# Two groups of four graphs at a time in layer 1's aggregation and weighted sum

## The chip, the cores and the metric

The kernel runs on one NeuronCore of a Trainium2 chip. The metric is the device time of one execution in microseconds (us), as a median over several runs; one further execution was recorded by the hardware profiler. The engines are TensorE (PE in the profile; its weight loads are PEld), VectorE (DVE), ScalarE (ACT), GpSimd (POOL) and SyncE (SP), which here only issues DMAs. [...]

## What is computed

128 graphs of 128 nodes with 256 features, all in fp32. Layer 0 is a gated network (convolution of 17 taps, messages between nodes, a GRU gate) on all nodes. Layer 1 works on the first 25 nodes only, in five overlapping groups of nodes, and is the part that is changed:

```python
GROUPS = [list(range(25)), list(range(9)), [0, 9, 10, 11, 12, 13, 14],
          [6, 7, 8, 12, 13, 14], [3, 4, 5, 9, 10, 11]]

def _graph_conv(x, adj, W, b):
    A = adj + eye(n)
    dinv = rowsum(A) ** -0.5            # 0 where the sum is 0
    norm_adj = dinv[:, :, None] * A * dinv[:, None, :]
    return relu(norm_adj @ (x @ W) + b)

h = relu(layernorm(x))
for g, idx in enumerate(GROUPS):
    hid = _graph_conv(h[:, idx], adj[:, idx][:, :, idx], W1[g], b1[g])    # 256 -> 512
    o = _graph_conv(hid, adj[:, idx][:, :, idx], W2[g], b2[g])            # 512 -> 256
    fused[:, idx] += softmax(fusion_w)[g] * o
x = x + fused
```

The changed steps are the second aggregation, `relu(norm_adj @ (...) + b2)`, and the weighted sum `fused`.

## The kernel before

The 53 pairs of a group and one of its nodes (25 + 9 + 7 + 6 + 6) are called rows; a graph has 64 row places, so two graphs fill 128 partitions. Layer 1 goes in 8 blocks of 16 graphs. A block has four **quads** of four graphs (`q` = 0 to 3). The steps of a block (`block`, from L1081) are:

- py (L1093): x1h, the normalized features, times the matrix r4 gathers and scales each graph's rows into `yz`, one step for each quad.
- `first(g)` and `second(g)` (L1110, L1119): the products with W1 and W2 for the five groups of nodes, over all 16 graphs. Group 0 has 25 nodes, so 400 columns.
- `turn(q)` (L1136): four transposes (L1141) bring the quad's rows to partitions, in one PSUM bank pzt; ACT copies them to SBUF as zt (L1145).
- `gather(q)` (L1147): four fp32 matmuls of 64 rows by 64 columns (L1153) apply the normalized adjacency `ac` of each graph. A pair of graphs is indexed by a, a graph in it by s. The results of s go to the left half of one PSUM bank pg2[s]. DVE adds b2 into zt for each s (L1156), ACT takes the relu of both (L1157).
- `fuse(q)` (L1159): two matmuls (L1163) with s2w, which holds the weights of the five groups, sum the rows of a graph onto its nodes; DVE adds the result to x1 (L1165), and x1's quad is stored: by one DMA of POOL (L1168) in blocks 0 to 6, in block 7 by four DMAs of one graph each (L1172), from SP or, for some, ACT.

Beside it, `prepare(blk)` makes the normalized adjacency and r4 of a later block; pa (L1042), dd (L1063), pg (L1068, 512 columns), pr (L1073) and the copies to r4 (L1077) are its steps. All of these take their PSUM banks from the pool `ptmp`, five banks in rotation; layer 0's last stage, `stage_c`, takes most of its own from `pgat`, three banks.

`stage_c` handles layer 0's gates for one group of four graphs at a time, 32 in all, as a series of products (L755) with sums and gates on DVE and ACT between them. Its last seven steps use the weight `wn` and end in two tanh (L884); its results are finished and turned by DVE (L918 to L929, L936) and, for the last group, through PE (po, L899, with the copies zr, L893).

The order of the instructions of all engines is laid down when the kernel is built, by the class `Order`. Several lanes hold generators. Each step of a generator issues its instructions and yields two numbers, a cost and a wait: the planner's clock advances by the cost, and the generator is not due again until the wait is over. Among the lanes that have something due, the one with the least cost done for its weight is taken; if none is due, the clock jumps to the earliest. In the last part of the kernel the lanes are:

```python
order.run(loads, groups, beside, Lane([fetch(q) for q in range(NQ)], ahead=2),
          Lane([rows(q) for q in range(NQ)], ahead=2),
          Lane(second, ahead=2, weight=0.2))
```

`groups` holds the 32 `stage_c`, `second` the series prepare(0), block(0), prepare(1), block(1) and so on, of which two run at a time. A block may start when its preparation is done and the block before has passed its last gather (`B1_DONE`). The products of the last `wn` steps yield a cost of 0.87 and a wait of 0.2.

Of the kernel before, what the change touches and what calls it, by code (L numbers as in the profile page):

```python
# [9 lines left out]
FP = mybir.dt.float32  # L10
AF = mybir.ActivationFunctionType
# [4 lines left out]
B, N, D = 128, 128, 256  # L16
# [3 lines left out]
P = 128  # L20
GB = 4
# [9 lines left out]
SB = 16  # L31
QS = SB // GB
NBLK = B // SB
# [7 lines left out]
RP = 64  # L41
WIDE = 32
# [165 lines left out]
def kernel(ctx: ExitStack, tc: tile.TileContext, x, adj, consts, vecs, w_se, conv1_w,  # L208
                    conv2_w, w_msg, b_msg, w_ih, w_hh, W1, W2, b2, fusion_w, out):
    nc = tc.nc  # L210
# [7 lines left out]
    ptmp = ctx.enter_context(tc.tile_pool(name="ptmp", bufs=5, space=PSUM))  # L218
# [19 lines left out]
    def v(name, i=None):  # L238
        a, b = VAT[name]
        return vec[:, a:b] if i is None else vec[:, a + i:a + i + 1]  # L240
# [17 lines left out]
    s2w = cp.tile([P, 2 * WIDE], FP, name="s2w")  # L258
# [106 lines left out]
    lab, turn = ExitStack(), []  # L365
# [624 lines left out]
    def load_w1(n):  # L990

        if n < NBLK * NG:
            S["w1", n] = S["pool"].tile([P, 2, HID], FP, tag="w1", name=f"w1_{n}", bufs=2)
            nc.sync.dma_start(out=S["w1", n], in_=W1[n % NG].rearrange("(k p) o -> p k o", p=P))
# [86 lines left out]
    def block(blk):  # L1081
        while not (blk in P_DONE and blk - 1 in B1_DONE):
            yield 0.0, 0.5
        pool, yz, b2row = S["pool"], S["yz"], S["b2row"]
        w2, ac, r4 = S["w2"], S["ac"][blk % 2], S["r4"][blk % 2]

        for q in range(QS):
            while blk * QS + q not in R_DONE:
                yield 0.0, 0.5
            x1h = S.pop(("x1h", blk * QS + q))  # L1090
            py = ptmp.tile([P, 2, GB, NR], FP, tag="tmp", name=f"py{blk}_{q}")
            for cc in range(2):
                nc.tensor.matmul(py[:, cc], x1h[:, cc * P:(cc + 1) * P],  # L1093
                                 r4[:, q].rearrange("p j r -> p (j r)"), start=True, stop=True)
            nc.vector.tensor_copy(yz[:, 0, q * GB:(q + 1) * GB, :NR], py[:, 0])  # L1095
            nc.scalar.activation(yz[:, 1, q * GB:(q + 1) * GB, :NR], py[:, 1], AF.Copy)
            PY_DONE.add(blk * QS + q)
            yield 0.75, 0.0 if q < QS - 1 else 2.4

        hs = {}  # L1100

        def first(g):
            n, o = SIZES[g], OFFS[g]
            w1 = S.pop(("w1", blk * NG + g))
            hh = hs[g] = pool.tile([P, 4, SB, n], FP, tag="hh0" if g == 0 else "hh",
                                   name=f"hh{blk}_{g}", bufs=1 if g == 0 else 2)
            for m in range(4):
                ph = ptmp.tile([P, SB, n], FP, tag="tmp", name=f"ph1{blk}_{g}_{m}")
                for k in range(2):
                    nc.tensor.matmul(ph, w1[:, k, m * P:(m + 1) * P],  # L1110
                                     yz[:, k, :, o:o + n], start=(k == 0), stop=(k == 1))
                nc.scalar.activation(hh[:, m], ph, AF.Relu, bias=v("b1", g * 4 + m))  # L1112

        def second(g):
            n, o = SIZES[g], OFFS[g]
            for cc in range(2):
                pz = ptmp.tile([P, SB, n], FP, tag="tmp", name=f"pz1{blk}_{g}_{cc}")
                for m in range(4):
                    nc.tensor.matmul(pz, w2[:, g, m, cc * P:(cc + 1) * P], hs[g][:, m],  # L1119
                                     start=(m == 0), stop=(m == 3))  # L1120
                nc.vector.tensor_copy(yz[:, cc, :, o:o + n], pz)  # L1121

        for g in range(NG + 1):
            if g < NG:
                first(g)
                yield 5.5 if g == 0 else 1.95, 0.0
            if g:
                second(g - 1)
                yield 5.5 if g == 1 else 1.95, 0.0 if g < NG else 1.0
            if g < NG:  # L1130
                load_w1(blk * NG + g + 2)
        x1 = X1[blk]

        zts = {}

        def turn(q):  # L1136
            pz = ptmp.tile([P, 2, D], FP, tag="tmp", name=f"pzt{blk}_{q}")
            for a in range(2):
                for cc in range(2):
                    b0 = q * GB + 2 * a  # L1140
                    nc.tensor.transpose(  # L1141
                        pz[:, a, cc * P:(cc + 1) * P],
                        yz[:, cc, b0:b0 + 2, :].rearrange("p s r -> p (s r)"), ident)
            zt = zts[q] = pool.tile([P, 2, D], FP, tag="zt", name=f"zt{blk}_{q}", bufs=4)
            nc.scalar.activation(zt, pz, AF.Copy)  # L1145

        def gather(q):  # L1147
            zt = zts[q]
            pg2 = [ptmp.tile([P, D], FP, tag="tmp", name=f"pg2{blk}_{q}_{s}") for s in range(2)]
            for a in range(2):  # L1150
                for s in range(2):
                    rows = slice(s * RP, (s + 1) * RP)
                    nc.tensor.matmul(pg2[s][a * RP:(a + 1) * RP], ac[rows, 2 * q + a],  # L1153
                                     zt[rows, a], start=True, stop=True)
            for s in range(2):
                nc.vector.tensor_add(zt[:, s], pg2[s], b2row)  # L1156
            nc.scalar.activation(zt, zt, AF.Relu)  # L1157

        def fuse(q):  # L1159
            zt = zts.pop(q)  # L1160
            pf = ptmp.tile([P, D], FP, tag="tmp", name=f"pfu{blk}_{q}")
            for s in range(2):
                nc.tensor.matmul(pf[s * 2 * WIDE:(s + 1) * 2 * WIDE], s2w, zt[:, s],  # L1163
                                 start=True, stop=True)
            nc.vector.tensor_add(x1[:, q], x1[:, q], pf)  # L1165
            b0 = blk * SB + q * GB
            if blk < NBLK - 1:
                nc.gpsimd.dma_start(out=out[b0:b0 + GB, :WIDE], in_=x1[:, q])  # L1168
                return
            for j in range(GB):  # L1170
                eng = nc.scalar if q == QS - 1 and j % 2 else nc.sync
                eng.dma_start(out=out[b0 + j, :WIDE], in_=x1[j * WIDE:(j + 1) * WIDE, q])  # L1172

        for what, q in ((turn, 0), (turn, 1), (turn, 2), (gather, 0), (turn, 3), (gather, 1),
                        (gather, 2), (fuse, 0), (gather, 3), (fuse, 1), (fuse, 2), (fuse, 3)):
            what(q)
            if (what, q) == (gather, QS - 1):
                B1_DONE.add(blk)
            yield {turn: 0.45, gather: 0.5, fuse: 0.5}[what], 0.5
        F_DONE.add(blk)  # L1180


# [23 lines left out]
    loads = Lane([stage_n(q) for q in range(NQ)])  # L1206
    groups = Lane([stage_c(q) for q in range(NQ)], ahead=2)
    second = [setup_1()] + [part(blk) for blk in range(NBLK) for part in (prepare, block)]
    beside.weight = 0.5
    order.run(loads, groups, beside, Lane([fetch(q) for q in range(NQ)], ahead=2),  # L1210
# [43 lines left out]
```

## Time and profile before

| | |
|---|---|
| median of 3 runs | 2012.26 us (2009.02 to 2017.96) |
| profiled execution | 2009.44 us, of it 2007.7 us from the first to the last instruction (the span) |
| granted TensorE clock in it | 0.997 |
| L1153, gather: 128 matmuls of 256 columns | two records each, 376 ns a record |
| L1156, b2 added: 64 of 128x256 | 416 ns each |
| L1157, relu: 32 of 128x512 | 630 ns each |
| L1163, weighted sum: 64 matmuls of 256 columns | two records each, 379 ns a record |
| L1165, x1 added: 32 of 128x256 | 415 ns each |
| block 0's first turn, block 7's last add | at 937.0 us, at 2001.0 us |

How to read it: an fp32 matmul appears as two records, whose ends are modelled and overlap with the next ones; what a matmul takes of the engine is read from the distance between starts. Line numbers are those of the kernel before. In a row of a timeline the columns are start, length from the first start to the last end (both us), engine, line, operation, output and inputs, shape and count; in brackets the engine's idle time and who ended it.

### The profile page before, as it was taken

Reading aid. Unit: us, or ns where it says so; the run is one execution under the profiler, and the core shown is the slowest. Engines: PE = TensorE matmul, PEld = TensorE weight load, DVE = VectorE, ACT = ScalarE, POOL = GpSimd, SP = SyncE. Lnnn points to the kernel's source line nnn. Section 1 sums busy time; section 2 is a strip of 40 time slices with the busy share of each in tenths; the row PEclk is TensorE's granted clock in tenths of the full one; section 3 lists DMA queues with packets and bytes.
Section 4 is the critical chain, followed back from the end, with each engine's and each line's share of the span. In section 5 each row is a group of like instructions: output and inputs, shape, how many; then the busy total and the mean of one; then the engine's idle time right before and its main releaser. Section 6 shows DMA issues by size and latency. Waiting matters only on the chain.

```text
span 2007.7 us, 33356 instructions
## 1 busy us (share of the span) xinstructions
PE 1960.1 (98%) x12598; PEld 1625.4 (81%) x12598; DVE 1352.3 (67%) x3002; ACT 683.4 (34%) x1547; POOL 655.7 (33%) x897
## 2 busy tenths in 40 slices
PE   7999999999999999999999999999999999999998
PEld 5667888889888888878778878888888888888865
DVE  6775445885433576885885787778668867886652
ACT  4664222454222344222323232232323332322233
POOL 3452666332656111241331232222221322222320
PEclk9999999999999999999999999999999999999999
DMA  9997879744887743542433342443442433433331
GB/s 212 296 273 250 274 250 289 220 148 158 269 258 254 198 124 107 163 103 82 119 90 108 106 113 77 118 112 88 118 121 80 126 102 98 107 102 108 65 94 53
DMA packets 184106, 302.88 MB, mean 151 GB/s; under 512 B 28501, under 2 KB 131994, under 8 KB 183690
## 3 DMA queue, kind: packets, MB, share of 16 engines
q1 hardware_dynamic: 138762, 168.81, 28.9%
q0 software_dynamic: 44800, 131.66, 22.6%
q8 instruction: 100, 1.64, 0.3%
q14 instruction: 60, 0.49, 0.1%
q10 hardware_dynamic: 384, 0.28, 0.1%
HBM read 204.12 MB, written 109.05 MB: 156 GB/s over the span
## 4 chain that ended last, share of the span: by engine, by line
PE 87%; DVE 7%; DMA 3%; issue 1%; ACT 1%; SPq 1%; POOL 0%; DVEq 0%; ACTq 0%; POOLq 0%
PE p L755 41%; PE pa L531 7%; PE ph L1110 5%; PE pz L1119 5%; PE pm L642 5%; PE pc L422 4%; PE pb L531 3%; PE px L668 3%; PE pf L433 3%; PE pi L712 3%; PE pw L477 1%; PE py L1093 1%; PE ph L411 1%; DMA xa<-in_x 1%; PE pse L626 1%
## 5 line engine op out<-in xcount | busy, mean ns | idle before, releaser
L938 POOL DMA_DIRECT2D x1d<-xt x128 | 101.1, 815 | 467.2 <-DVE xt L936 454.9
L837 POOL DMA_DIRECT2D xt<-in_x x128 | 100.2, 789 | 173.8 <-DMA x1d<-xt 166.8
L563 DVE SCALAR_TENSOR_TENSOR y<-pa,kk 128x512 f32<-128x512 f32 x78 | 53.8, 690 | 151.2 <-ACT kk L562 151.1
L531 PE MATMUL pa<-wf,X 128*128 128x256 f32 x640 | 152.2, 381 | 0.0
L755 PE MATMUL p<-th,wrz 128*128 128x256 f32 x512 | 134.5, 385 | 0.0
L755 PE MATMUL p<-tc,wrz 128*128 128x256 f32 x512 | 131.4, 379 | 0.0
L755 PE MATMUL p<-tm,wrz 128*128 128x256 f32 x512 | 131.4, 379 | 0.0
L531 PEld LDWEIGHTS pa<-wf,X 128*128 128x128 f32 x640 | 118.1, 190 | 16.2 <-issue 2.0
L422 PE MATMUL pc<-c1w,hTa 128*128 128x256 f32 x512 | 121.2, 383 | 2.7 <-DVE X L439 1.5
L642 PE MATMUL pm<-wmsg,hT 128*128 128x256 f32 x512 | 121.5, 382 | 0.0
L1110 PE MATMUL ph<-yz,w 128*128 128x96 f32 (+3 forms) x640 | 109.3, 325 | 1.4 <-DVE yz L1095 1.4
L422 PEld LDWEIGHTS pc<-c1w,hTa 128*128 128x128 f32 x512 | 94.0, 191 | 19.9 <-DVE h L425 4.8
L755 PEld LDWEIGHTS p<-th,wrz 128*128 128x128 f32 x512 | 94.7, 190 | 19.1 <-issue 7.3
L1112 ACT ACTIVATE hh<-ph,vec 128x96 f32<-128x96 f32 (+3 forms) x160 | 63.6, 401 | 133.5 <-PE ph L1110 125.1
L724 ACT ACTIVATE xc<-xc,t_bn 128x256 f32<-128x256 f32 x128 | 58.2, 500 | 148.5 <-DVE xc L721 148.5
L755 PEld LDWEIGHTS p<-tc,wrz 128*128 128x128 f32 x512 | 97.3, 190 | 13.9 <-issue 0.8
L642 PEld LDWEIGHTS pm<-wmsg,hT 128*128 128x128 f32 x512 | 95.8, 190 | 15.2 <-ACT kk L562 1.4
L1119 PE MATMUL pz<-hh,w 128*128 128x96 f32 (+3 forms) x640 | 107.5, 322 | 0.7 <-DVE yz L1121 0.7
L755 PEld LDWEIGHTS p<-tm,wrz 128*128 128x128 f32 x512 | 97.3, 190 | 13.2
L1110 PEld LDWEIGHTS ph<-yz,w 128*128 128x128 f32 x640 | 88.3, 193 | 22.4 <-issue 15.6
L1119 PEld LDWEIGHTS pz<-hh,w 128*128 128x128 f32 x640 | 86.3, 191 | 18.6 <-DVE yz L1121 1.3
L755 PE MATMUL p<-hTc,wrz 128*128 128x256 f32 x384 | 99.3, 381 | 1.2 <-DVE z L829 1.2
(204 smaller groups left out, 4464.8 us busy)
## 6 DMA issues: line engine op xcount, KB each, us to landing
wf<-wfd SPq DMA_DIRECT2D x160, 256.0 KB
wfd<-ws POOLq DMA_DIRECT2D x64, 320.0 KB, 10.2
yd<-y POOLq DMA_DIRECT2D x80, 256.0 KB, 4.0
yt<-yd SPq DMA_DIRECT2D x64, 320.0 KB
w<-in_W SPq DMA_DIRECT2D x40, 512.0 KB
xa<-in_x SPq DMA_DIRECT2D x128, 128.0 KB
hTd<-hTa POOLq DMA_DIRECT2D x32, 512.0 KB, 6.6
hT<-hTd SPq DMA_DIRECT2D x32, 512.0 KB
```

The costliest lines, as they stand in the source:

```text
L422: nc.tensor.matmul(pc[:, i], hT[:, k, (2 * h + i) * N:(2 * h + i + 1) * N], c1w[:, k], start=(k == 0), stop=(k == 1))
L433: nc.tensor.matmul(pf[:, i, :F * NB], h1[:, 2 * h + i, k * P:(k + 1) * P], fwd, start=True, stop=True)
L531: nc.tensor.matmul(ps, xk(k), WF[f][:, k, s], start=(k == 0), stop=(k == 1))
L642: nc.tensor.matmul(pm[:, i], hT[:, k, j * N:(j + 1) * N], LATE["wmsg"][:, k], start=(k == 0), stop=(k == 1))
L668: nc.tensor.matmul(px[:, dc, i], msgs[h][:, i, dc * P:(dc + 1) * P], aT[:, 2 * h + i], start=True, stop=True)
L712: nc.tensor.matmul(pi[w * WIDE:(w + 1) * WIDE, :, :, n].rearrange("p k g c -> p g k c"), inv[:F, o:o + WIDE], yt[:, n // 2::2].rearrange(" ...
L755: nc.tensor.matmul(ps[:, m], w[:, i, k, m * P:(m + 1) * P], factor(i, x, t), start=first and j == 0, stop=last and j == len(n) - 1, skip_g ...
L837: nc.gpsimd.dma_start(out=xt[a * WIDE:(a + 1) * WIDE].rearrange("p b d c -> p (b d) c"), in_=slices(x[q * GB:(q + 1) * GB])[a])
L938: nc.gpsimd.dma_start(out=slices(x1d[q])[a], in_=xt[a * WIDE:(a + 1) * WIDE].rearrange("p b d c -> p (b d) c"))
L1110: nc.tensor.matmul(ph, w1[:, k, m * P:(m + 1) * P], yz[:, k, :, o:o + n], start=(k == 0), stop=(k == 1))
L1112: nc.scalar.activation(hh[:, m], ph, AF.Relu, bias=v("b1", g * 4 + m))
L1119: nc.tensor.matmul(pz, w2[:, g, m, cc * P:(cc + 1) * P], hs[g][:, m], start=(m == 0), stop=(m == 3))
```

## The change

`gather` and `fuse` work on two quads (h = 0, 1) in place of one. Two turns write into one SBUF tile zt of twice the size (two of them instead of four). A gather makes eight matmuls, with the results of s now filling the whole bank pg2[s]; then for each s one add of 512 columns and one relu of 512 columns. A fuse makes two matmuls of 512 columns, which fill one whole bank, and one add of 512 columns; then the two quads' stores are issued. In block 7 the odd graphs of both last quads (not of the last one alone) are stored from ACT's queue. The order within a block's end has eight steps in place of twelve; a double gather and a double fuse yield a cost of 1.0 in place of 0.5, and a gather a wait of 1.5 in place of 0.5.

```diff
-            zt = zts[q] = pool.tile([P, 2, D], FP, tag="zt", name=f"zt{blk}_{q}", bufs=4)
-            nc.scalar.activation(zt, pz, AF.Copy)
-
-        def gather(q):
-            zt = zts[q]
-            pg2 = [ptmp.tile([P, D], FP, tag="tmp", name=f"pg2{blk}_{q}_{s}") for s in range(2)]
-            for a in range(2):
-                for s in range(2):
-                    rows = slice(s * RP, (s + 1) * RP)
-                    nc.tensor.matmul(pg2[s][a * RP:(a + 1) * RP], ac[rows, 2 * q + a],
-                                     zt[rows, a], start=True, stop=True)
+            if q % 2 == 0:
+                zts[q // 2] = pool.tile([P, 2, 2, D], FP, tag="zt", name=f"zt{blk}_{q}", bufs=2)
+            nc.scalar.activation(zts[q // 2][:, q % 2], pz, AF.Copy)
+
+        def gather(h):
+            zt = zts[h]
+            pg2 = [ptmp.tile([P, 2, D], FP, tag="tmp", name=f"pg2{blk}_{h}_{s}")
+                   for s in range(2)]
+            for i in range(2):
+                for a in range(2):
+                    for s in range(2):
+                        rows = slice(s * RP, (s + 1) * RP)
+                        nc.tensor.matmul(pg2[s][a * RP:(a + 1) * RP, i], ac[rows, 4 * h + 2 * i + a],
+                                         zt[rows, i, a], start=True, stop=True)
             for s in range(2):
-                nc.vector.tensor_add(zt[:, s], pg2[s], b2row)
-            nc.scalar.activation(zt, zt, AF.Relu)
-
-        def fuse(q):
-            zt = zts.pop(q)
-            pf = ptmp.tile([P, D], FP, tag="tmp", name=f"pfu{blk}_{q}")
+                nc.vector.tensor_add(zt[:, :, s], pg2[s],
+                                     b2row[:, None, :].to_broadcast([P, 2, D]))
+                nc.scalar.activation(zt[:, :, s], zt[:, :, s], AF.Relu)
+
+        def fuse(h):
+            zt = zts.pop(h)
+            pf = ptmp.tile([P, 2, D], FP, tag="tmp", name=f"pfu{blk}_{h}")
             for s in range(2):
-                nc.tensor.matmul(pf[s * 2 * WIDE:(s + 1) * 2 * WIDE], s2w, zt[:, s],
+                nc.tensor.matmul(pf[s * 2 * WIDE:(s + 1) * 2 * WIDE], s2w, zt[:, :, s],
                                  start=True, stop=True)
-            nc.vector.tensor_add(x1[:, q], x1[:, q], pf)
...
+            nc.vector.tensor_add(x1[:, 2 * h:2 * h + 2], x1[:, 2 * h:2 * h + 2], pf)
+            for q in (2 * h, 2 * h + 1):
...
+                for j in range(GB):
+                    eng = nc.scalar if q >= QS - 2 and j % 2 else nc.sync
+                    eng.dma_start(out=out[b0 + j, :WIDE], in_=x1[j * WIDE:(j + 1) * WIDE, q])
 
         for what, q in ((turn, 0), (turn, 1), (turn, 2), (gather, 0), (turn, 3), (gather, 1),
-                        (gather, 2), (fuse, 0), (gather, 3), (fuse, 1), (fuse, 2), (fuse, 3)):
+                        (fuse, 0), (fuse, 1)):
             what(q)
-            if (what, q) == (gather, QS - 1):
+            if (what, q) == (gather, 1):
                 B1_DONE.add(blk)
-            yield {turn: 0.45, gather: 0.5, fuse: 0.5}[what], 0.5
+            yield {turn: 0.45, gather: 1.0, fuse: 1.0}[what], 1.5 if what is gather else 0.5
```

More of the change, by code (lines that the diff above doesn't have):

```diff
@@ L1162, in fuse @@
+        def fuse(h):
+            zt = zts.pop(h)
+            pf = ptmp.tile([P, 2, D], FP, tag="tmp", name=f"pfu{blk}_{h}")
             for s in range(2):
-                nc.tensor.matmul(pf[s * 2 * WIDE:(s + 1) * 2 * WIDE], s2w, zt[:, s],
+                nc.tensor.matmul(pf[s * 2 * WIDE:(s + 1) * 2 * WIDE], s2w, zt[:, :, s],
                                  start=True, stop=True)
[L1165 to L1169, printed above, removed]
@@ L1170, in fuse @@
-            for j in range(GB):
-                eng = nc.scalar if q == QS - 1 and j % 2 else nc.sync
-                eng.dma_start(out=out[b0 + j, :WIDE], in_=x1[j * WIDE:(j + 1) * WIDE, q])
+            nc.vector.tensor_add(x1[:, 2 * h:2 * h + 2], x1[:, 2 * h:2 * h + 2], pf)
+            for q in (2 * h, 2 * h + 1):
+                b0 = blk * SB + q * GB
+                if blk < NBLK - 1:
+                    nc.gpsimd.dma_start(out=out[b0:b0 + GB, :WIDE], in_=x1[:, q])
+                    continue
+                for j in range(GB):
+                    eng = nc.scalar if q >= QS - 2 and j % 2 else nc.sync
+                    eng.dma_start(out=out[b0 + j, :WIDE], in_=x1[j * WIDE:(j + 1) * WIDE, q])
```

## The prediction

> **What bounds the kernel now.** I read the page, then busy time by window, then TensorE's own timeline, then the chain of waits at the end. The page:
>
> ```profile
> span 2007.7 us, 33356 instructions
> PE 1960.1 (98%) x12598; PEld 1625.4 (81%) x12598; DVE 1352.3 (67%) x3002; ACT 683.4 (34%) x1547; POOL 655.7 (33%) x897
> ```
>
> By window (columns: stretch, length, busy us and instructions of PE, PEld, DVE, ACT, POOL, granted clock, DMA share, GB/s):
>
> ```profile
> 1500.00:1700.00 200.00, 200.00 (x1286) 167.33 (x1285) 155.55 (x340) 58.98 (x127) 54.42 (x77) 1.00 0.39 106
> 1700.00:1911.50 211.50, 211.50 (x1332) 176.33 (x1331) 158.25 (x337) 61.64 (x135) 56.34 (x80) 1.00 0.37 94
> 1911.50:1925.60 14.10, 10.43 (x71) 5.91 (x69) 13.24 (x37) 5.41 (x11) 3.42 (x6) 1.00 0.08 17
> 1993.50:2007.70 14.20, 6.56 (x63) 3.41 (x63) 4.34 (x12) 4.58 (x8) 0.00 (x0) 0.89 0.16 38
> ```
>
> From 930 us until layer 0's last group ends at 1913.5, TensorE never rests: only its own time counts there. Behind that end DVE is the full engine (13.24 of 14.10 us), and in the last stretch nobody is: that is latency. The changed steps lie in all three. TensorE's timeline in layer 1's second block (start, us; two matmul records are one fp32 matmul):
>
> ```profile
> 1159.69 0.66 PE L1153 MATMUL pg<-zt,ac 64*64 64x256 f32 x8
> 1160.29 0.70 PE L755 MATMUL p<-xm,wn 128*128 128x256 f32 x2
> 1160.82 0.59 PE L755 MATMUL p<-xc,wn 128*128 128x256 f32 x2
> 1161.35 0.66 PE L1153 MATMUL pg<-zt,ac 64*64 64x256 f32 x8
> 1161.94 0.70 PE L755 MATMUL p<-tm,wn 128*128 128x256 f32 x2
> 1162.48 0.59 PE L755 MATMUL p<-tc,wn 128*128 128x256 f32 x2
> 1163.00 0.65 PE L1163 MATMUL pfu<-zt,s2w 128*64 128x256 f32 x4
> 1163.58 0.70 PE L755 MATMUL p<-tm,wn 128*128 128x256 f32 x2
> ...
> 1164.64 0.66 PE L1153 MATMUL pg<-zt,ac 64*64 64x256 f32 x8
> ```
>
> A layer-0 product takes 0.435 us (four records from 1141.45 to 1142.32). From gather to gather is 1.66 us with two products in it: a lone gather costs 1.66 - 0.87 = **0.79 us**. A lone fuse costs 1.64 - 0.87 = **0.77 us**. Side by side they are cheaper:
>
> ```profile
> 1913.60 1.09 PE L1153 MATMUL pg<-zt,ac 64*64 64x256 f32 x16
> 1914.62 0.65 PE L1163 MATMUL pfu<-zt,s2w 128*64 128x256 f32 x4
> ```
>
> Two gathers take 1.02 us to the next start, one alone 0.60 (1160.29 less 1159.69): the second adds 0.42 to 0.43. So each visit to the small tiles costs 0.79 - 0.43 = 0.36 us beyond its work (fuse: 0.34). In blocks 0 to 4 all 40 gathers and fuses stand alone.
>
> [...] 416 ns for 256 columns (L1156), 687 for 512 (L425, same operands)[...]. [...] L1068 shows 512 columns at 0.86 us, twice a product, so width costs nothing extra.
>
> **Part by part, against the profiled execution's 2009.44 us (span 2007.7).**
>
> *A. Fewer visits, blocks 0 to 4.* Per block four gather steps become two of eight matmuls, four fuse steps two of two 512-column matmuls. Each pairing saves one visit: 10 x 0.36 + 10 x 0.34 = **-7.0 us**, all where TensorE is full. Bounds: 0 [...] to -7.0.
>
> *B. The order.* `Order` knows only yielded costs and waits, so I replayed its rule on those alone; for the kernel before, the replay gives the sequence the trace shows (block 5: turn 1, prepare, turn 2, gather 0, prepare, turn 3 between the last group's products; then gather 1, 2, fuse 0, gather 3, py). The `wn` steps of each group wait 0.2 behind themselves, and layer 1's steps slip into those holes, one per hole. A block's end needed twelve holes; now eight steps, plus about two holes skipped during the longer wait of 1.5 after a gather. So layer 1 runs ahead. Replayed: block 5's gather and fuse steps and py 0 to 2 of block 6 are placed before the last group begins; py 3, `first(0)`, `first(1)`, `second(0)` of block 6 stand between its last products. Before, gather 1 to 3, all fuses, po and four py (L1093) fill the DVE-bound stretch from 1913.50 to 1925.64 = 12.14 us. Inside the full phase the same work costs: a double gather 1.22, two fuses 2.40, four py at 0.72 (1166.20 to 1166.92), 0.43 for the first gather's second half, and po 0.41: 7.34. **-4.8 us**. What is late next: the last group's own end. From its last product to zr takes about 6.0 us (two tanh 1.4, six ops of L918-920 4.2, copies 0.4); the replay puts first 2, second 1, first 3, second 2 and prepare's pa before po, about 9.2 us of PE by their rows. Covered; without that cover it would cost up to 6.
>
> *C. End of block 6.* Now pg (L1068) falls before the second gather and pr (L1073) before the last fuse. Row by row: first gather done 1956.4, two adds of 0.69 to 1957.9, pg 1957.0 to 1957.9, ac 1958.7, ACT's two relus (L1157, 0.63) and then the last turn's copy to 1959.1, gather's second half to 1959.7, fuse 1960.6, pr 1961.5, r copies (1.5 us) to 1963.3, py at 1963.35 against 1963.91: **-0.5 us**. Bounds -1 to +1.6 (py behind the last fuse as well).
>
> *D. End of block 7.* The chain of waits before:
>
> ```profile
> 1995.53 0.59 PE pzt L1141 x4
> 1996.12 0.66 PE pg L1153 x8
> ...
> 1997.41 0.65 PE pfu L1163 x4
> ...
> 1999.62 0.64 ACT zt L1157
> ...
> 2001.04 0.42 DVE x L1165
> ```
>
> Behind it SP issues 14 stores from 1998.61 to 2005.03, and these end the kernel. The change makes the last copy (L1145) stand in ACT's queue behind both relus of the first gather, which wait for adds of 0.69 each; the second gather, in TensorE's queue, waits for that copy. First gather done 1995.96; adds to 1997.38; relus 1996.86 to 1998.10; copy to 1998.59; gather's second half to 1999.35; adds to 2000.77; first fuse's add, queued behind them, to 2001.38. SP starts at 2001.42: 2.8 later, with twelve issues instead of 14 (two go to ACT): 2 x 0.46 back, part of one odd 0.87 us issue too. **+1.6 us**, bounds +0.9 to +2.8.
>
> *At nothing.* DVE: 96 adds of 0.416 become 48 of 0.69, 6.8 us less, hidden by TensorE except inside B. ACT: as many copies and relus. POOL's stores: same 28, twice two per add; behind them wait L938 and pow, on an engine 33% busy. PSUM: ten bank takes per block instead of 16. New stalls in the full phase: 0 to +22, see the rivals; I take 0.
>
> **Sum**: -7.0 - 4.8 - 0.5 + 1.6 = **-10.7 us**, 1998.7 for that execution. It lies 2.8 below the median of 2012.26, so the forecast for the median is 2001.5.
>
> **Rivals.** *1, the order brings nothing* (B is 0, because `first(0)` between the last products stalls by as much): -5.9, 2006.4. For it: the last products and their tanh chain lengthen by 13 us of foreign work. Against: that work is full-speed matmul.
>
> *2, slower.* TensorE outruns its banks: in the six last `wn` steps of a group DVE has some 5.4 us of work (by rows: 9 of 0.42, 2 of 0.48, one of 0.69) for 6 x 0.87 = 5.2 us of products. The full phase already shows three such stalls on r L877, the longest 1.80 us. A gather now holds DVE for its 1.22 us of PE and then 1.38 us of adds. If each of the 12 early gathers brought such a stall: +21.6, together +10.9, 2023.2. It decides from about 0.9 us per gather. Against: turns and fuses give DVE air, and four waits on zt L1156 cost PEld 1.4 us and PE nothing.
>
> *3, more*: those three stalls vanish through DVE's 6.8 us: -14, 1998.3.
>
> *4*: copies that wait as in D in the full phase too. The 1.5 wait puts two products ahead, so at most 1 us a block; it is in the range.
>
> **How the numbers follow.** Half a per cent, 10 us, is about what a measurement of this kernel can tell from no change. Main case 0.70, with its parts between -6 and -14: just over half beyond it, 0.45 faster, 0.25 same. Rival 1 0.10: 0.02, 0.08. Rival 2 0.12: 0.01 same, 0.11 slower. Rival 3 0.08: faster. Sum: faster 0.55, same 0.34, slower 0.11. Range 1993 to 2012: from the main case with rival 3 and all bounds at their good end, to no gain; rival 2 is left out. The main case's own range is 1998 to 2007.
>
> **What would show it.** A: PE's matmuls 64 records fewer, L1163's replacement with 512 columns, double gathers of about 1.02 us. B: block 6's 400-column matmuls ahead of the last group's tanh, and no stretch with DVE full and PE at three quarters behind it. D: first store some 8 us before the end instead of 9, and the ACT copy behind two relus. Wrong: PE idle before L755 on DVE above 10 us, or block 6 starting behind the last group.

## The result, and the profile after

| | before | after |
|---|---|---|
| median, 22 runs each, same chip | 2014.11 us (2006.29 to 2021.11) | 2006.12 us (1999.18 to 2021.02) |
| ratio, as recorded (the medians' quotient is 0.9960) | | 0.9965, 95% interval 0.995 to 0.998 |
| profiled execution, span | 2009.44, 2007.7 us | 2006.22, 2004.4 us |

The change brings about 7 us (0.35% of 2014; by the interval 4 to 10), where 10.7 was forecast. In the kernel after, the turn's copy is L1146, gather L1156, its adds L1159, relus L1161, fuse L1167, the add to x1 L1169, the stores L1173 (POOL) and L1177.

The page after (busy us, share, count of each engine), beside the two lines of before's page in the prediction:

```profile
span 2004.4 us, 33141 instructions
PE 1958.2 (98%) x12534; PEld 1628.8 (81%) x12534; DVE 1345.2 (67%) x2954; ACT 683.0 (34%) x1547; POOL 654.5 (33%) x897
```

PE has 64 records fewer, DVE 48 instructions and 7.1 us fewer: the counts of the plan. By window (the columns as before). The bounds lie at block 6's first 400-column product, at the end of layer 0's last product (1930.80), and at the second transpose of block 6 and of block 7, where a block's turns begin to follow each other closely:

```profile
1700.00:1915.46 215.46, 215.46 (x1344) 181.63 (x1343) 162.61 (x343) 64.10 (x140) 59.47 (x85) 1.00 0.38 94
1915.46:1930.80 15.34, 15.34 (x61) 10.28 (x60) 4.29 (x12) 3.89 (x8) 3.46 (x9) 1.00 0.39 105
1930.80:1949.44 18.64, 17.38 (x134) 16.72 (x132) 10.84 (x33) 5.33 (x15) 2.57 (x4) 0.91 0.29 85
1988.72:2004.40 15.68, 6.96 (x55) 3.07 (x55) 3.86 (x6) 4.51 (x8) 0.00 (x0) 0.89 0.14 34
```

The stretch with DVE full and PE at three quarters is gone: behind layer 0's end PE is busy 17.38 of 18.64 us. New is a clock of 0.91 there. TensorE's timeline around one double gather and double fuse of the second block:

```profile
1161.93 0.59 PE L755 MATMUL p<-tc,wn 128*128 128x256 f32 x2
1162.45 1.09 PE L1156 MATMUL pg<-zt,ac 64*64 64x256 f32 x16
1163.48 0.70 PE L755 MATMUL p<-xm,wn 128*128 128x256 f32 x2
...
1164.44 0.88 PE L1093 MATMUL py<-r,x1h 128*128 128x212 f32 x4
...
1166.12 1.08 PE L1167 MATMUL pfu<-zt,s2w 128*64 128x512 f32 x4
1167.13 0.70 PE L755 MATMUL p<-tm,wn 128*128 128x256 f32 x2
...
1168.09 0.88 PE L1093 MATMUL py<-r,x1h 128*128 128x212 f32 x4
```

The product before the gather needs TensorE until 1161.93 + 0.43; from there to the start of py are 2.08 us. Less the two products between (0.435 each), the double gather takes 1.21 us; forecast 1.22. Around layer 0's end:

```profile
1915.46 5.58 PE L1110 MATMUL ph<-yz,w 128*128 128x400 f32 x16
...
1930.37 0.59 PE L755 MATMUL p<-xc,wn 128*128 128x256 f32 x2
...
1934.13 1.25 PE L1119 MATMUL pz<-hh,w 128*128 128x144 f32 x8 [0.40 <-DVE yz L1121]
...
1938.87 1.99 PE L1042 MATMUL pa<-cst,b 25*128 25x64 f32 x16
...
1941.71 0.41 PE L899 MATMUL po<-cst,zr 128*128 128x128 f32 x2 [0.61 <-DVE zr L893]
```

Block 6's 400-column products stand 15 us ahead of the last layer-0 product, as replayed; po still waits 0.61 us for zr. The chain of waits at the end:

```profile
1991.29 0.70 DVE zt L1159
1991.99 0.02 issue
1992.01 1.23 ACT zt L1161 x2
1993.23 0.49 ACT zt L1146
1993.73 0.04 issue
1993.77 0.73 PE pg L1156 x8
```

The ACT copy (L1146, done at 1993.73) stands behind both relus (1.23 us), and the second half of the last gather starts behind it, at 1993.77, after 1.43 us of PE waiting: step D as foretold. SP's first store comes at 1996.46, 7.9 us before the end.

**Where the time went.** The part of the program up to block 0's first 400-column product is the same in both kernels, yet its length in the records of kernels that leave it alone runs from 901.8 (e1 below) to 918.2 us (e2). So two single records are compared from that product on ("affected part"), in us, with the ends of the spans rounded to 0.1:

| stretch | before | after | difference |
|---|---|---|---|
| first 400-column product to block 6's second transpose | 1046.40 | 1038.67 | -7.73 |
| to block 7's first product (C) | 13.48 | 13.25 | -0.23 |
| block 7's products | 26.03 | 26.03 | 0 |
| from block 7's second transpose (D) | 14.18 | 15.68 | +1.50 |
| affected part | 1100.09 | 1093.63 | -6.46 |

One more thing differs. The clock column shows **dips**, stretches of 3.41 us or a multiple at half the clock. Up to TensorE's last matmul, before has one in the affected part, after has two. The windows view of after, up to a dip and within it:

```profile
1461.00:1465.00 4.00, 4.00 (x27) 3.27 (x27) 1.71 (x5) 1.17 (x3) 3.22 (x5) 1.00 0.32 66
1465.00:1468.40 3.40, 3.40 (x16) 3.22 (x15) 2.81 (x11) 0.00 (x0) 3.22 (x5) 0.50 0.86 170
```

PE is busy throughout, at clock 0.50. An estimate from these two figures: half of 3.41 us, 1.71, is lost where PE is full (1.72 in the comparison with e8 below). Without dips the parts are 1098.4 and 1090.2: -8.2 us. "At full clock" below means this reckoning, 1.71 off for each 3.41 us of dip; it takes off too much where TensorE would have waited anyway.

### The profile page after: what moved, and what is told of

Read it like the earlier page. It is cut to its first block, busy times and chain, and to the rows that moved or that the text cites. A ratio compares the mean times of both kernels' runs of the same rounds, so it can differ in the third digit from the quotient of the medians.

```text
span 2004.4 us, 33141 instructions
## 1 busy us (share of the span) xinstructions
PE 1958.2 (98%) x12534; PEld 1628.8 (81%) x12534; DVE 1345.2 (67%) x2954; ACT 683.0 (34%) x1547; POOL 654.5 (33%) x897
## 4 chain that ended last, share of the span: by engine, by line
PE 88%; DVE 7%; DMA 2%; ACT 1%; issue 1%; SPq 1%; DVEq 0%; POOL 0%; ACTq 0%; POOLq 0%
PE p L755 41%; PE pa L531 7%; PE pz L1119 5%; PE ph L1110 5%; PE pm L642 5%; PE pc L422 4%; PE pb L531 3%; PE pf L433 3%; PE px L668 3%; PE pi L712 3%; PE pw L477 1%; PE ph L411 1%; PE py L1093 1%; DMA xa<-in_x 1%; PE pse L626 1%
## 5 line engine op out<-in xcount | busy, mean ns | idle before, releaser
L755 PE MATMUL p<-th,wrz 128*128 128x256 f32 x512 | 135.5, 387 | 0.0
L755 PE MATMUL p<-tm,wrz 128*128 128x256 f32 x512 | 132.0, 380 | 0.0
L755 PE MATMUL p<-tc,wrz 128*128 128x256 f32 x512 | 131.4, 379 | 0.0
L755 PEld LDWEIGHTS p<-th,wrz 128*128 128x128 f32 x512 | 95.0, 191 | 18.8 <-issue 6.0
L755 PEld LDWEIGHTS p<-tm,wrz 128*128 128x128 f32 x512 | 97.9, 191 | 13.5
L755 PEld LDWEIGHTS p<-tc,wrz 128*128 128x128 f32 x512 | 97.3, 190 | 13.9 <-issue 0.8
L755 PE MATMUL p<-hTc,wrz 128*128 128x256 f32 x384 | 99.1, 381 | 1.3 <-DVE z L829 1.3
```

Of the source, the lines that this page charges most:

```text
L755: nc.tensor.matmul(ps[:, m], w[:, i, k, m * P:(m + 1) * P], factor(i, x, t), start=first and j == 0, stop=last and j == len(n) - 1, skip_g ...
```

## The experiments

**The kernels once more (again, before_again).** Nothing is edited. After:

> The changed kernel once more, unaltered. Measure: the affected part, from block 0's first matmul of 400 columns to the last instruction, 1100.1 us before and 1093.6 after. Theory (the order decides): the part is 1093.6 again to within 0.5, with the same six waits of PE on DVE in the full phase (5.0 us). The granted clock halved for 3.4 us from about 12 us behind the last group's last product. If that belongs to the order (small pa matmuls, then a wait at po), it is there again; if it is chance, it is missing or elsewhere, and the part is 1.7 us shorter, 1091.9.

Measured: 2011.4 us, affected part 1098.83, with six dips' worth (at 934.6, 1019.9, 1467.1, 1811.8 and a double one at 1944.9). At full clock 1088.6, which is 1.6 less than the first record's 1090.2: so far apart can the reckoning put two records of one kernel. The order is that of the first record; of its waits on DVE in the full phase, 5.0 us, the one of 0.7 before pr is missing (4.2 us). Dips behind prepare's pa recur at two of the same places; their number does not repeat. Before:

> The kernel before once more, unaltered. The profiles so far show stretches in which the granted clock is halved, a multiple of 3.41 us long; each costs up to 1.71 us where TensorE is full. In the affected part (block 0's first 400-column matmul to the end) there was one in the kernel before, two in the changed one, six in its repeat. Theory: their number is chance of the execution; the affected part less 1.71 us for each is 1098.4 here again to within 1, and their number may be anything from 0 to 6. Rival: the narrow steps and the old order keep the clock up; there are 0 to 1 again, and the dips are a cost of the change.

Measured: 2007.94 us, affected part 1100.36, one dip again, at 1269.0 (1270.8 in the first record). At full clock 1098.65.

**Wide steps at the old pace (e1_wide_old_pace).** The double steps are kept; twelve yields with the old costs and waits are restored (`skip` does nothing).

```diff
...
-        for what, q in ((turn, 0), (turn, 1), (turn, 2), (gather, 0), (turn, 3), (gather, 1),
-                        (fuse, 0), (fuse, 1)):
+        for what, q, cost in ((turn, 0, 0.45), (turn, 1, 0.45), (turn, 2, 0.45), (skip, 0, 0.5),
+                              (turn, 3, 0.45), (gather, 0, 0.5), (skip, 0, 0.5), (skip, 0, 0.5),
+                              (gather, 1, 0.5), (fuse, 0, 0.5), (skip, 0, 0.5), (fuse, 1, 0.5)):
...
-            yield {turn: 0.45, gather: 1.0, fuse: 1.0}[what], 1.5 if what is gather else 0.5
+            yield cost, 0.5
```

> Wide gathers and fuses, in the slots of the order before: the dropped steps remain as empty steps that yield the old costs and waits. Theory (a visit to the small tiles costs 0.36 us, the rest is order): from block 0's first 400-column matmul to the end of layer 0's last product 1005.9 before becomes 998.1 (7.0 for 20 visits, 0.8 for block 5's first gather that falls behind the end); DVE-bound stretch behind it stays, 12 to 13 us; end of the kernel +0.5 (the last turn's copy is ahead of the relus here); affected part 1093.5. Rival ([...] wide instructions save nothing in PE): 1005.1 to the end of the last product, affected part 1100.5.

Measured: 2004.42 us; affected part 1100.83 with six dips' worth. Up to the end of layer 0's last product 1002.74 us, less three dips (5.1) 997.6; before 1005.89 less one 1004.2: -6.6 us. Of it 0.8 is block 5's first gather, which here falls behind that product; against it TensorE's waits in the full phase are 5.2 us, 0.9 more than before's 4.3 (shown with e4 below). Without both, step A is **-6.7 us** (forecast -7.0). It can be read without a reckoning between the first 400-column products of blocks 1 and 2, where neither record has a dip or a wait (first before, then e1):

```profile
1057.78 5.59 PE L1110 MATMUL ph<-yz,w 128*128 128x400 f32 x16
1228.40 5.58 PE L1110 MATMUL ph<-yz,w 128*128 128x400 f32 x16
```

```profile
1056.30 5.58 PE L1110 MATMUL ph<-yz,w 128*128 128x400 f32 x16
1225.50 5.58 PE L1110 MATMUL ph<-yz,w 128*128 128x400 f32 x16
```

170.62 us become 169.20: 1.42 less for four visits fewer, where the prediction's prices give 1.40. Between blocks 3 and 4, and 4 and 5, it is 1.22 and 1.43. The cost is paid per visit, not per weight load: two single gathers take 2 x 0.79 us, a double one 1.21 in the record of after, with the same eight matmuls; both records hold 256 weight loads of gathers. The window behind layer 0's last product has the DVE-bound stretch back:

```profile
1904.50:1917.61 13.11, 9.55 (x60) 5.09 (x59) 11.70 (x28) 4.97 (x11) 3.44 (x5) 0.90 0.03 4
```

To block 6's second transpose at full clock: 997.6 + 13.1 + 28.4 (the stretch after it, as before has it) = 1039.1, of which a dip in the window may be 1.0; after 1038.67 less two dips is 1035.25. The new pace brings 2.9 to 3.9 us there. But e1 has 12.44 and 14.48 us in the next two stretches, after 13.25 and 15.68: about 2 us go back. Over the whole affected part e1 stands at 1090.6 us at full clock, beside 1090.2 and 1088.6 in the two records of after: of what the new pace gains, 0.4 to 2 us are left.

**Narrow steps at the new pace (e2_narrow_new_pace).** The functions are those of before; each step calls two.

```diff
...
+        for what, qs in ((turn, (0,)), (turn, (1,)), (turn, (2,)), (gather, (0, 1)), (turn, (3,)),
+                         (gather, (2, 3)), (fuse, (0, 1)), (fuse, (2, 3))):
+            for q in qs:
+                what(q)
...
```

> The narrow gathers and fuses of before, two back to back in one step, with the new order's costs and waits. Theory (a step's visit and the order are all; width is worth nothing to PE): PE's time to the end of the last product as after, 1020.0 to within 1; block 6 starts before the last group ends; affected part 1093.6 to within 1.5. Rival (the wide banks pay: 48 fewer adds, 6.8 us of DVE, 32 fewer matmuls): at least 3 us longer, 1096.6 or more.

Measured: 2014.2 us, of it 918.18 in the unchanged part; affected part 1094.22 with three dips, 1089.1 at full clock. Its TensorE timeline, a fuse pair of four 256-column matmuls:

```profile
1174.28 0.59 PE L755 MATMUL p<-tc,wn 128*128 128x256 f32 x2
1174.81 1.08 PE L1163 MATMUL pfu<-zt,s2w 128*64 128x256 f32 x8
1175.82 0.70 PE L755 MATMUL p<-tm,wn 128*128 128x256 f32 x2
1176.36 0.59 PE L755 MATMUL p<-tc,wn 128*128 128x256 f32 x2
```

1.01 us to the next start, as with two of 512 columns (1167.13 less 1166.12). Filling whole banks saves TensorE nothing here; standing side by side does: from the product ahead of the pair (1174.28) to the second one behind it (1176.36) are 2.08 us, so the pair costs 1.21, two products off, where two lone fuses cost 2 x 0.77.

**The last turn ahead of the first gather in block 7 (e3_last_turn_first).**

```diff
...
+        if blk == NBLK - 1:
+            steps[3:5] = steps[4], steps[3]
...
```

> As after, but in block 7 alone the fourth turn stands ahead of the first gather, so that its copy is ahead of the relus in ACT's queue. Theory (that queue cost the 1.5 us at the end): wait of 1.43 us of PE on zt gone, first store 0.8 us earlier, last stretch from 15.7 to 14.9, affected part 1092.8. Rival (the adds of 512 columns and the double fuse set the end): no change, 15.7. The full phase is the same as after; it also shows whether the clock dip comes back.

Measured: 2007.65 us; from the second transpose of block 7 14.52 us instead of 15.68 (-1.16), affected part 1098.71 with six dips' worth. Its chain at the end:

```profile
1994.38 0.70 DVE zt L1159
1995.08 0.02 issue
1995.11 0.64 ACT zt L1161
1995.74 0.04 issue
1995.79 2.88 PE pfu L1167 x8
```

The copy is out of the chain, one add (0.70 us) and one relu (0.64) remain, and PE's 1.43 us of waiting is gone. Step D's mechanism is shown.

**Copies from DVE to ACT (e4_copies_on_act).** The kernel after, with the copies to r4 and half of those of pz on ACT.

```diff
-            nc.vector.tensor_copy(r4[s, :, j % 2 * 2 + j // 2, :], pr4[s, :, j % 2, :NR])
+            nc.scalar.activation(r4[s, :, j % 2 * 2 + j // 2, :], pr4[s, :, j % 2, :NR], AF.Copy)
...
-                nc.vector.tensor_copy(yz[:, cc, :, o:o + n], pz)
+                if cc:
+                    nc.scalar.activation(yz[:, cc, :, o:o + n], pz, AF.Copy)
+                else:
+                    nc.vector.tensor_copy(yz[:, cc, :, o:o + n], pz)
```

> As after, with prepare's copies to r4 and half of second's copies to yz on ACT in place of DVE (48 fewer on DVE, some 20 us). Theory (PE's waits in the full phase come from DVE's backlog): those of 5.0 us fall by half or more, the 0.40 us on yz and the 0.61 us before po shrink; affected part at full clock 1086.5 to 1088 against 1088.6 to 1090.2. Rival (ACT's queue makes these copies later than DVE did): waits on ACT take their place, 1090 or more.

Measured: 1995.65 us; affected part 1090.32 with two dips, 1086.9 at full clock (1090.2 and 1088.6 in the records of after). The waits of TensorE in the full phase (engine, line waited for: us, times, longest), first of before, then of after, then of e4, where the last line lies behind the full phase:

```profile
PE p L755 <- DVE r L877: 3.3, 3, 1.8
PE py L1093 <- ACT x1h L1011: 1.0, 1, 1.0
```

```profile
PE p L755 <- DVE r L877: 2.7, 4, 0.9
PE p L755 <- DVE r L869: 1.6, 1, 1.6
PE pr L1073 <- DVE ac L1069: 0.7, 1, 0.7
```

```profile
PE p L755 <- DVE r L877: 1.8, 3, 0.6
PE p L755 <- DVE r L869: 1.4, 1, 1.4
PE pz L1119 <- DVE yz L1124: 0.4, 1, 0.4
```

5.0 us become 3.2, less of a cut than expected. Of it, the 4.3 us before L755 fall to 3.2; the 0.7 before pr is missing in the unedited repeat too, so its absence proves nothing. The wait of 0.40 us for yz behind layer 0's end stays. po no longer waits for zr (0.61 us in after), and from layer 0's last product to block 6's second transpose pass 16.37 us (17.00 with no dip and the copies on DVE, in e6 below). So DVE's queue held po, and a part of the waits before L755.

**Block 6's end, and a POOL store (e5_end).** As e3 in blocks 6 and 7; besides, the first quad of block 7 is stored whole by POOL, so SP issues eight stores.

```diff
-                if blk < NBLK - 1:
+                if blk < NBLK - 1 or q == 0:
...
+        if blk >= NBLK - 2:
+            steps[3:5] = steps[4], steps[3]
...
```

> As after, with the fourth turn ahead of the first gather in blocks 6 and 7, and block 7's first quad stored by one DMA of POOL instead of four of SP. Theory (ACT's queue and SP's row of stores set the end): end of block 6 from 13.25 to 12.6; last stretch, 15.67 in after and 14.52 with the turn alone, to 12.7 (four issues of 0.46 fewer on SP). Rival (the POOL store lands last, some 4.5 us behind its issue): 14 or more.

Measured: 2005.57 us. Stretch C is 12.49 us instead of 13.25, as expected; the end is 14.97, worse than e3's 14.52. The waits of SP's queue:

```profile
SPq L1177 <- DVE x L1169: 17.6, 1, 17.6
SPq L1177 <- DMA out<-x: 1.6, 1, 1.6
```

Four issues fewer did not help: SP stood 1.6 us for a store to finish, and POOL issued its one only at 1996.36; it landed at 2001.28, 4.9 us later, while SP's last issue came at 2000.38. The end is the one that the rival foretold (14 or more). Whether POOL's store or SP's last one landed last, and so what set the end, this record doesn't show, and no run separates it.

**Prepare's pa over all 128 rows, after and before (e6_full_rows, e8_before_full_rows).** In the records of before, after and again, every dip from block 0's pa to the end of TensorE's work, 2, 3 and 5 of them, begins 2.2 to 4.0 us after the start of a pa: before's at 1270.8 follows pa at 1268.03, after's at 1465.0 and 1942.9 follow pa at 1462.30 and 1938.87. Each pa is eight matmuls of 25 rows by 64 columns, 1.83 us of PE. They are given 128 rows, the added ones zero.

```diff
-        S["b1"] = pool.tile([NN, SB, RP], FP, name="b1")
+        S["b1"] = pool.tile([P, SB, RP], FP, name="b1")
...
-                             c("et")[:NN, :RP], start=True, stop=True)
+                             c("et")[:, :RP], start=True, stop=True)
```

(The other uses of `b1` keep to its first 25 rows; the rest stay at zero from its first memset.)

> The kernel after, with prepare's pa matmuls (L1042, 25 rows, 64 columns, eight of them, 1.8 us) over all 128 rows, the added ones zero. Nothing else moves. Theory (the half-clock dips of 3.4 us that stand behind pa come from these nearly empty matmuls): no dip behind any pa; those elsewhere stay; the part from block 0's first 400-column matmul to the end about 1090 us if there is no dip, against 1093.6 in the profile of after with two. Median 1 to 4 us under after, ratio 0.994 to 0.996. Rival (dips depend on the phase of PE's waits, and zero rows count as little): dips at about 1465 and 1943 again, ratio as after's 0.9965.

> The kernel before, with prepare's pa matmuls over all 128 rows and nothing else. Theory: the one dip that both records of before show, at about 1270 behind a pa, is gone: affected part 1098.4 us instead of 1100.1 to 1100.4, ratio about 0.999 (1 to 2 us). Rival: the dip stays or others come, ratio 1.000.

Measured, beside 27 runs of before (median 2012.94): after with full rows 2001.64 us (6 runs), ratio **0.9936** (0.9917 to 0.9955); before with full rows 2009.06 (22 runs), ratio **0.9976** (0.9963 to 0.9988). No dip stands behind any of the eight pa in either record. Before's two (one of them, at 874.8, ahead of the affected part) are gone, and so are after's (877.9, 1465.0, 1942.9). Before's dip, and then the same place behind pa in e8:

```profile
1270.75:1274.18 3.43, 3.43 (x16) 3.25 (x15) 2.60 (x9) 0.71 (x2) 2.23 (x3) 0.50 0.43 104
```

```profile
1269.08:1272.51 3.43, 3.43 (x26) 3.27 (x25) 2.63 (x10) 1.42 (x4) 2.64 (x4) 1.00 0.61 141
```

From block 2's first 400-column product to block 3's are 190.88 us before and 189.16 in e8, so this dip cost 1.72. Over all records, 29 of the 72 pa with 25 rows (nine records) have a dip that begins 2.2 to 4.2 us after their start; of the 24 with full rows (e6, e8 and e7 below) none has. The windows view of e6 from layer 0's last product to block 6's second transpose:

```profile
1923.49:1940.49 17.00, 15.71 (x134) 15.09 (x132) 10.82 (x33) 5.35 (x15) 2.57 (x4) 1.00 0.30 93
```

17.00 us at clock 1.00, against 18.64 at 0.91. The affected part of e8 is 1098.66, what the reckoning at full clock gave for before (1098.4, 1098.65). That of e6 is 1091.54 with one dip, at 1004.6, which has another companion: the timeline shows PE idle right ahead of it.

```profile
1001.55 0.59 PE L755 MATMUL p<-tc,wn 128*128 128x256 f32 x2
1004.82 1.22 PE L755 MATMUL p<-tm,wn 128*128 128x256 f32 x2 [2.67 <-DVE r L869]
```

That 2.67 us is the same wait of TensorE for DVE as after's 1.6. One dip each of e1, e2 and e3 (at 1915.0, 1018.6 and 1010.6) stands behind such waits too, of 2.30, 2.01 and 1.67 us, and behind no pa; e5's wait of 1.8 brought none. The rival, that phase decides and zero rows count as little, falls. Whether it is the rows or the smaller tile that the clock answers to, these runs do not separate.

**All together (e7_all).** The kernel after with full rows, e4's copies and the turn ahead of the gather in blocks 6 and 7.

> The kernel after, with full rows for pa as in e6, the copies to r4 and half of the copies of pz moved from DVE to ACT, and the fourth turn ahead of the first gather in blocks 6 and 7. Theory: the single gains add: full-phase waits of PE before L755 on DVE about 3.2 us instead of 5.0; 16.4 us behind layer 0's last product instead of 18.6; end 14.5 instead of 15.7; affected part about 1086 us, ratio to before 0.992 to 0.9945. Rival (the gains hide each other, or the early part of the kernel decides by its own spread): 0.996 or more.

Measured: 1993.29 us (6 runs), ratio **0.9907** (0.9885 to 0.9929): the fastest of all. Affected part 1085.66 us, no dip until TensorE has ended. Waits of PE on DVE in the full phase 3.4 us before L755 and 0.6 before pr, 16.33 us behind layer 0's last product, 12.23 in stretch C, 14.45 at the end. The ratio is lower than the 0.992 expected at best, though its interval reaches it; the affected part is as expected, so the gains add.

## Why the prediction was right, and where it was off

The direction held, and the size within the stated range: -10.7 us forecast, about -7 measured (ratio 0.9965). Step by step, at full clock:

- **A, visits.** Forecast -7.0; e1 measured -6.7. Right, and e2 shows the reason: steps side by side pay for one visit, whatever their width (a fuse pair takes 1.01 us with 256 columns and with 512). What TensorE does in the 0.36 us of a visit was not shown. The bound of 0, where all the cost comes with the weight loads, falls: a double gather, with as many weight loads, costs 1.21 us against 2 x 0.79.
- **B, the order.** The replayed order is the trace's. A and B together measured -9.4 (1044.7 to 1035.25) of the forecast -11.8; with e1's A, B is about -2.7 of -4.8, where e1 against after gives 2.9 to 3.9. The term that was mis-sized is "new stalls, 0" together with "covered": behind layer 0's end came 0.40 and 0.61 us that were not in the sum. The waits in the full phase were 5.0 us in after's record and 4.3 in before's (the views above; TensorE did not quite "never rest" from 930 us on), but 4.2 in after's repeat and 5.2 in e1 at the old pace, so the new order is not shown to have added any there. That leaves 0.4 to 1.1 us of the gap unassigned.
- **The cover of po.** The sum gave zr 6.0 us from the last product. It took 10.9 (1930.80 to 1941.7), longer than the 9.2 us of PE work in front. DVE's timeline shows why:

```profile
1931.35 1.27 DVE L1036 TENSOR_REDUCE dg<-b 25x16 f32<-25x400 f32 x5
1933.77 0.31 DVE L1121 COPY yz<-pz 128x144 f32<-128x144 f32 x1 [1.15 <-PE pz L1119]
1935.42 0.31 DVE L1121 COPY yz<-pz 128x144 f32<-128x144 f32 x1 [1.34 <-PE pz L1119]
1935.64 0.68 DVE L918 TENSOR_TENSOR hTc<-hTc,r 128x512 f32<-128x512 f32 x1
```

  DVE took these in the order of its queue. L918, the chain's first, starts at 1935.64, behind the reduces of prepare (1.27 us from first to last) and two copies of yz, which wait 1.15 and 1.34 us for their products on TensorE. The forecast added up the chain's own instructions and left out those that the new order puts between them.
- **C.** Forecast -0.5, measured -0.23, within its bounds.
- **D.** Forecast +1.6, measured +1.50; e3 took 1.16 of it away, so for the reason given in the main.
- **Dips.** No step had them. After's record had one more than before's in the affected part, which turns -8.2 at full clock into -6.46. The runs of after, and all those beside e6 and e8, are on record with their mean clock, rounded to 0.001 (2 us of a run). If each run's time is multiplied by its clock, the 22 runs of after lie within 8 us of each other instead of 22, and the 27 of before beside e8 within 9 instead of 22: most of the spread between runs is the clock's. The medians so reckoned are 2002.8 us for before and 1993.1 for after, an estimate of -9.7 us for the change, nearer to the forecast than -7. For e8 it is 2002.2, so the gain of e8 over before is the clock's too. With full rows on both sides, e6 and e8, the medians differ by 7.4 us, the affected parts by 7.1, or by 8.8 at full clock.

Of the rivals, the first (the order brings nothing) gave 2006.4, nearer to the measured 2006.12 than the forecast. That is luck: e1 shows that the order did shorten the part up to block 6's second transpose, and what is missing from the forecast is in part dips, which the rival did not have either. The second (DVE's backlog stalls every gather) fell: 4.2 to 5.0 us of waits in the full phase, where before had 4.3 and the rival asked for 22 more; "wrong" was set at 10 us of waits before L755 on DVE, and there were 4.3. The third (the old stalls vanish) fell: they moved, and one at L869 is new. The fourth, copies that wait in the full phase, left no wait of PE in that view.

## What to carry to other kernels

On a full TensorE, count the visits to a small tile shape, not the width of the work: pairs standing side by side save 0.34 to 0.36 us each here, in one bank or two. When such a pairing shifts the order, re-add every in-order queue that the moved steps share with the chain behind them, with the waits of the foreign instructions, and not the chain's own operations alone. And look at the granted clock before explaining single microseconds between two records: one dip of 3.43 us at 0.50 cost 1.72 us here.

## What the hardware showed that was not expected

The granted clock fell to 0.50 for 3.41 us at a time, also where TensorE had no idle time at all (after's dip at 1465.0: busy 3.40 of 3.40 us, and 4.00 of the 4.00 us ahead of it), mostly right behind eight matmuls of 25 rows by 64 columns (1.83 us): 29 of 72 such pa have a dip behind them. What lowers the clock inside the chip was not shown. What the runs show is that a dip came behind these nearly empty matmuls without any wait of TensorE, as at 1465.0, and that with zeros in the empty rows none of 24 pa had one, in all three kernels tried. The time on TensorE stayed nearly the same (pa and the product behind it 2.16 us in after, 2.20 with full rows in e8), and the kernel before got 0.24% shorter (0.12 to 0.37).
